# A GAT layer and a top-p attention layer on one core: layer 1's output shift added in layer 0, and single-column operations given from VectorE to GpSimd

## The chip, the cores and the metric

The kernel runs on one core of a Trainium2 chip. Its time is the device time of one execution in microseconds (us). A core has five engines that run at the same time, each with its own instruction queue that it works through in order: TensorE (PE, matrix products, whose weight loads are listed apart as PEld), VectorE (DVE), ScalarE (ACT), GpSimd (POOL) and SyncE (SP, which here issues DMA transfers only). An instruction that needs another engine's result waits on a semaphore, and everything behind it in its own queue waits with it. GpSimd also issues DMA transfers, from the same queue as its arithmetic.

## The reference

Two layers over a graph of 3327 nodes with 256 features. Layer 0 is a graph attention layer with four heads and a projection; layer 1 takes a normalised copy `h` of its result through two steps of a graph walk and of a sparse attention, sums them, normalises, scales by `ln_g`, shifts by `ln_b`, and adds the result to what came in:

```python
h = relu(layernorm(x))
x = x + gat(h, adj, weight, weight_u, weight_v, bias, proj_w, proj_b)     # layer 0
h = relu(layernorm(x))                                                    # layer 1
R = (adj + I) / row_sums
Z, Xf, Xa = 0, h, h
for n in range(2):
    A = top_p(softmax((Xa @ W1.T @ W2.T) @ (Xa @ W3.T).T))
    Xf = R @ Xf
    Xa = A @ Xa
    Z = Z + Xf @ U1[n].T + Xa @ U2[n].T
out = x + layernorm(h + Z) * ln_g + ln_b
```

`top_p` keeps in each row the largest probabilities until they reach 0.9 of the row's sum, sets the rest to zero and divides the row by what is kept.

## The kernel before

The 3327 nodes are 26 row tiles of 128 (the last has 127).

**Layer 0** goes through the transposed adjacency in four blocks of columns: three of 1024 and a narrow one of 255. In each of a block's 26 steps VectorE makes four weight tiles (`weigh`, L570, one for each head, into seven buffers `w`), two before and two after the other VectorE work of that step, and TensorE multiplies them with the features (`sum_features`, L578) and with a column for the denominators (`sum_weights`, L588). A block's 8 row tiles are finished while the next block runs, one every three steps; the last block's two are finished at the end of the layer. Finishing a tile is the class `Out`: TensorE transposes the sums (L437), VectorE's `normalize` divides them and adds the residue (L445 to L451: this is `x1`, the input of layer 1's residue), stores `x1` to `x1_d`, and takes its mean and variance (L457, L459); GpSimd makes the scale and the shift of the norm (L461 to L463), ScalarE applies them (L464: `h`), and TensorE turns `h` (L473) and makes queries and keys (L483) and the features of the graph walk (L506). VectorE comes back in `take_keys` (L178) and `take_graph` (L517). GpSimd also copies the adjacency to `adj_r` by DMA.

**Layer 1** runs two steps (s = 0 and 1) over the 26 row tiles. Several tiles are in work at once: `m` (logits and exponentials), `a` (search of the threshold), `b` (the cut), `c` (transposes and the product), `d` (storing). The order in which their parts are issued is written out by hand in `PLANS`: for each step one plan for the fill, one for the steady part and one for the drain. The word `graph` there stands for a share of the graph walk, four row tiles of the adjacency (L742, L743), with which TensorE is filled. After the program is built, the order of TensorE, VectorE, ScalarE and GpSimd is fixed as it was issued.

For one row tile: TensorE makes the logits (L799); VectorE and ScalarE copy them to SBUF (L810); ScalarE takes the exponentials and their sum (`exp`, L822, after GpSimd's three constants at L820); GpSimd works out a first guess of the threshold in 22 operations on single columns (`guess`, L838 to L859, whose L846 is what the first probe needs); ScalarE probes it four times (`probe`, L880; after the first, `go_on`, L888 and L889, makes the next point `at`). After each of the other probes VectorE narrows the bracket (`narrow`, L902 to L924); at the first narrowing it first sets the bracket's ends (L899). Then ScalarE makes the threshold (L930). VectorE sums what lies below it (`low`, L937, one pass over the row of 3327, its sum `below`), takes the largest eight of eight segments (`largest`, L946) and finds the last value that is kept (`last_kept`, L954 to L970): the sum of the row less `below` (L959, `sums[:, :1]`) starts a running sum (L960). GpSimd checks that the cut is certain (`make_sure`, L977 to L980). VectorE zeroes the rest of the row (`keep`, L985) and takes the reciprocal `rk` of what is kept (L989). TensorE transposes the row (L998), VectorE and ScalarE copy it back (L1008), TensorE multiplies it with the features (L1019), and VectorE scales by `rk`: in step 0 to `nxa` (L1037), from which TensorE makes the next step's features, in step 1 to the output's sum (L1040). The output is then normalised: VectorE takes mean and variance (L156, L158), adds epsilon (L160), GpSimd raises to -1/2 (L162), and VectorE applies mean and `ln_g` (L1082), then the scale and the residue `x1`, read back from `x1_d` (L1085), and the shift `ln_b` (L1086).

Between the two steps, `load_graph` reads the graph features of step 1 with 18 DMA transfers issued by GpSimd (`move_rows` with GpSimd's queue, L145). They are issued at the head of the iteration in which the last row tile is `b` and the one before it `c`; each waits for the stores of its part and for the buffer. `mean_of_keys` (L262) needs the keys of step 1, read back by SP as `k_sb` (L246).

In the fill plan of step 0 `b.keep` stands before `m.guess`; in all other plans with a guess it stands after it.

Of the kernel before, what the change touches and what calls it, by code (L numbers as in the profile page):

```python
# [10 lines left out]
FP = mybir.dt.float32  # L11
# [5 lines left out]
ALU = mybir.AluOpType  # L17
# [4 lines left out]
P = 128  # L22
D = 256
DC = D // P
# [3 lines left out]
DA = 64  # L28
# [26 lines left out]
def kernel(  # L55
# [85 lines left out]
    def move_rows(queue, dst, src, pn):  # L141

        for p0, p1 in ((0, pn // 16 * 16), (pn // 16 * 16, pn)):
            if p0 < p1:
                queue.dma_start(out=dst[p0:p1], in_=src[p0:p1])  # L145

    def row_of(pool, src, name, queue=nc.sync, tag=None):

        t = pool.tile([P, D], FP, tag=tag or name, name=name)
        queue.dma_start(out=t, in_=src.partition_broadcast(P))  # L150
        return t

    def mean_and_rstd(src, pn):

        st = small.tile([P, 6], FP, tag="ln_st", name="ln_st")
        nc.vector.bn_stats(st[:pn], src[:pn])  # L156
        mv = small.tile([P, 2], FP, tag="ln_mv", name="ln_mv")
        nc.vector.bn_aggr(mv[:pn], st[:pn])  # L158
        ve = small.tile([P, 1], FP, tag="ln_ve", name="ln_ve")
        nc.vector.tensor_scalar(ve[:pn], mv[:pn, 1:2], EPS, None, ALU.add)  # L160
        rs = small.tile([P, 1], FP, tag="ln_rs", name="ln_rs")
        nc.gpsimd.tensor_tensor(rs[:pn], ve[:pn], mhalf[:pn], ALU.pow)  # L162
        return mv, rs
# [138 lines left out]
    with ExitStack() as l0:  # L302
# [26 lines left out]
        load_x(4, 8)  # L329
        badd = row_of(p0, bias, "badd", nc.gpsimd)  # L330
        pb = row_of(pa, proj_b, "pb", nc.gpsimd, tag="xu")
        for g0 in range(8, NT, 4):
            load_x(g0, min(g0 + 4, NT))
        w1_sb = p0.tile([P, DC, DA], FP, name="w1_sb")
# [95 lines left out]
        class Out:  # L430
# [10 lines left out]
            def normalize(r):  # L441
                pn, i, pt = r.pn, r.i, r.pt
                rden = small.tile([P, H], FP, tag="rden", name="rden")

                nc.vector.tensor_scalar(rden[:pn], pt[:pn, HP, ::QP], 1.0 / BIG, None, ALU.max)  # L445
                nc.vector.reciprocal(rden[:pn], rden[:pn])
                x1 = pa.tile([P, D], FP, tag="x1", name="x1")
                for h in range(H):
                    hs = slice(h * O, (h + 1) * O)
                    q0 = (h % 2) * O  # L450
                    nc.vector.scalar_tensor_tensor(  # L451
                        x1[:pn, hs], pt[:pn, h // 2, q0 : q0 + O], rden[:pn, h : h + 1],
                        res[:pn, i, hs], ALU.mult, ALU.add,
                    )
                move_rows(nc.sync, x1_d[r.n0 : r.n0 + pn], x1, pn)
                st = small.tile([P, 6], FP, tag="ln_st", name="ln_st")
                nc.vector.bn_stats(st[:pn], x1[:pn])  # L457
                m = small.tile([P, 4], FP, tag="ln_m", name="ln_m")
                nc.vector.bn_aggr(m[:pn, :2], st[:pn])  # L459
                g = nc.gpsimd  # L460
                g.tensor_scalar(m[:pn, 2:3], m[:pn, 1:2], EPS, None, ALU.add)  # L461
                g.tensor_tensor(m[:pn, 2:3], m[:pn, 2:3], mhalf[:pn], ALU.pow)
                g.tensor_scalar(m[:pn, 3:], m[:pn, :1], -1.0, m[:pn, 2:3], ALU.mult, ALU.mult)  # L463
                nc.scalar.activation(  # L464
                    res[:pn, i], x1[:pn], AF.Relu, bias=m[:pn, 3:], scale=m[:pn, 2:3]
                )
                move_rows(nc.sync, h_d[r.n0 : r.n0 + pn], res[:, i], pn)
# [80 lines left out]
            features(i, (7, 1)[i % 2])  # L548
            take(i)

        w1n = p0.tile([DA, DC, P], FP, name="w1n")
        pt = bank(2, [P, DC, P])
        for c in range(DC):
            nc.tensor.transpose(pt[:DA, c, :], w1_sb[:, c, :], ident)
# [141 lines left out]

    pl = ctx.enter_context(tc.tile_pool(name="pl", bufs=1))
    lng = row_of(pl, ln_g, "lng")
    lnb = row_of(pl, ln_b, "lnb")

    def load_nodes(xa, s, g):

# [68 lines left out]
    class Rows:  # L771
# [113 lines left out]
        def go_on(r):  # L885

            pn = r.pn
            nc.scalar.activation(r.g[:pn], r.g[:pn], AF.Copy, scale=half)  # L888
            nc.scalar.activation(  # L889
                r.at[:pn, 4:], r.g[:pn], AF.Identity, bias=r.step[:pn], scale=r.per_g[:pn]  # L890
            )

        def narrow(r, j):

            pn = r.pn
            if j == 1:
                nc.vector.tensor_scalar(  # L899
                    r.ends[:pn, :, 1], far[:pn], r.at[:pn, 4:], None, ALU.add  # L900
                )
            nc.vector.scalar_tensor_tensor(  # L902
                r.at[:pn, 1:4:2], r.g[:pn].to_broadcast([pn, 2]), half,
                r.ea[:pn].to_broadcast([pn, 2]), ALU.mult, ALU.mult,
            )
            mk = small.tile([P, 2], U32, tag="mk", name="mk")
            nc.vector.tensor_tensor(mk[:pn], r.at[:pn, 1:3], r.at[:pn, 0:2], ALU.is_ge)
            nc.vector.copy_predicated(
                r.ends[:pn],
                mk[:pn].unsqueeze(2).to_broadcast([pn, 2, 2]),  # L910
                r.at[:pn, 3:].unsqueeze(1).to_broadcast([pn, 2, 2]),
            )
            fhi, nhi = r.ends[:pn, 1, :1], r.ends[:pn, 1, 1:]
            t = small.tile([P, 4], FP, tag="t", name="t")
            short, gap, w = t[:pn, :1], t[:pn, 1:3], t[:pn, 3:]
            nc.vector.tensor_tensor(gap, r.ends[:pn, 0], r.ends[:pn, 1], ALU.subtract)
            nc.vector.tensor_scalar(short, r.aims[0][:pn], fhi, 0.0, ALU.subtract, ALU.max)
            if j == PROBES - 1:
                nc.vector.scalar_tensor_tensor(
                    short, r.aims[1][:pn], fhi, short, ALU.is_gt, ALU.mult  # L920
                )
            nc.vector.reciprocal(w, gap[:, :1])
            nc.vector.scalar_tensor_tensor(w, gap[:, 1:], w, short, ALU.mult, ALU.mult)  # L923
            nc.vector.tensor_tensor(r.at[:pn, 4:], w, nhi, ALU.add)  # L924
# [9 lines left out]
        def low(r):  # L934
            pn, e = r.pn, r.e[: r.pn]
            r.below = small.tile([P, 1], FP, tag="below", name="below")
            nc.vector.scalar_tensor_tensor(  # L937
                r.lg[:pn, :N], e, r.th[:pn], e, ALU.is_lt, ALU.mult, accum_out=r.below[:pn]
            )

        def largest(r):

# [5 lines left out]
        def last_kept(r):  # L948
            pn = r.pn
            v8 = r.v8[:pn].rearrange("p s v -> p (s v)")  # L950
            v = small.tile([P, WINDOW], FP, tag="v", name="v", bufs=1)
            top = small.tile([P, 1], FP, tag="top", name="top")

            nc.vector.tensor_reduce(top[:pn], r.v8[:pn, :, 7], AX.X, ALU.max)  # L954
            nc.vector.max(v[:pn, :8], v8)
            nc.vector.match_replace(v8, v[:pn, :8], v8, -1.0)
            nc.vector.max(v[:pn, 8:], v8)
            sums = small.tile([P, WINDOW + 1], FP, tag="sums", name="sums", bufs=2)
            nc.vector.tensor_tensor(sums[:pn, :1], r.ssum[:pn], r.below[:pn], ALU.subtract)  # L959
            nc.vector.tensor_tensor_scan(  # L960
                sums[:pn, 1:], v[:pn], v[:pn], sums[:pn, :1], ALU.add, ALU.max
            )
            ends = small.tile([P, 2, WINDOW], FP, tag="vends", name="vends", bufs=1)
            for j in range(2):
                nc.vector.scalar_tensor_tensor(
                    ends[:pn, j], sums[:pn, j : j + WINDOW], r.tgt[:pn], v[:pn],
                    ALU.is_ge, ALU.mult,
                )
            r.vm = small.tile([P, 2], FP, tag="vm", name="vm")
            nc.vector.tensor_reduce(r.vm[:pn], ends[:pn], AX.X, ALU.max)  # L970
            r.found = sums, top
# [10 lines left out]
        def keep(r):  # L982
            pn, e = r.pn, r.e[: r.pn]
            kept = small.tile([P, 1], FP, tag="kept", name="kept")
            nc.vector.scalar_tensor_tensor(  # L985
                e, e, r.vm[:pn, 1:], e, ALU.is_ge, ALU.mult, accum_out=kept[:pn]
            )
            r.rk = small.tile([P, 1], FP, tag="rk", name="rk", bufs=4)
            nc.vector.reciprocal(r.rk[:pn], kept[:pn])  # L989


        def transpose(r, *groups):
# [87 lines left out]
        def store_output(r):  # L1080
            pn, zt = r.pn, r.zt[: r.pn]
            nc.vector.scalar_tensor_tensor(  # L1082
                zt, zt, r.mv[:pn, 0:1], lng[:pn], ALU.subtract, ALU.mult
            )
            nc.vector.scalar_tensor_tensor(zt, zt, r.rs[:pn], r.x1[:pn], ALU.mult, ALU.add)  # L1085
            nc.vector.tensor_add(zt, zt, lnb[:pn])  # L1086
            move_rows(nc.sync, out[r.n0 : r.n0 + pn], zt, pn)

    def general_cut(i, s, k_sb, pows):
# [387 lines left out]
```

## Time and profile before

| | us |
|---|---|
| median of 3 runs | 2095.51 |
| lowest and highest | 2094.33, 2095.57 |
| the profiled execution | 2095.06 |
| its span | 2092.8 |
| TensorE busy (95% of the span) | 1985.8 |
| VectorE busy (82%) | 1715.9 |
| ScalarE busy (60%) | 1265.2 |
| GpSimd busy (38%) | 787.5 |

The span is what the profiler's instructions cover; the rest of the execution's time lies around it. A row of a timeline gives start, duration, engine, line, operation, output and inputs, a count where rows are merged, and in brackets the time that the engine had been idle and what ended the wait. Matmuls overlap, so the busy time of TensorE is not a measure of how well it is used, but its idle time is time in which it had nothing to do. The column of the clock is the share of its full clock that TensorE was granted.

### The profile page before, as it was taken

Reading aid. Unit: us, or ns where it says so; the run is one execution under the profiler, and the core shown is the slowest. Engines: PE = TensorE matmul, PEld = TensorE weight load, DVE = VectorE, ACT = ScalarE, POOL = GpSimd, SP = SyncE. Lnnn points to the kernel's source line nnn. Section 1 sums busy time; section 2 is a strip of 40 time slices with the busy share of each in tenths; the row PEclk is TensorE's granted clock in tenths of the full one; section 3 lists DMA queues with packets and bytes.
Section 4 is the critical chain, followed back from the end, with each engine's and each line's share of the span. In section 5 each row is a group of like instructions: output and inputs, shape, how many; then the busy total and the mean of one; then the engine's idle time right before and its main releaser. Section 6 shows DMA issues by size and latency. Waiting matters only on the chain. (4 is left out here: it accounts for less than half of the span.)

```text
span 2092.8 us, 34266 instructions
## 1 busy us (share of the span) xinstructions
PE 1985.8 (95%) x11474; PEld 1387.5 (66%) x11474; DVE 1715.9 (82%) x4065; ACT 1265.2 (60%) x1940; POOL 787.5 (38%) x1834
## 2 busy tenths in 40 slices
PE   6999999999999679999999999998899999999996
PEld 3333223323333468888888888876798898888885
DVE  4777888878877388888888888864899999999995
ACT  2110000000012588888888888847899999999982
POOL 2330033223233233444444444432555444554441
PEclk9999999999999889999999999999899999999998
DMA  5455555655645433333333333377334443334420
GB/s 173 146 174 170 161 196 190 229 175 183 217 131 175 130 81 91 102 100 98 102 102 103 100 103 103 101 224 197 77 99 102 118 105 102 101 99 111 107 73 20
DMA packets 319569, 270.60 MB, mean 129 GB/s; under 512 B 30168, under 2 KB 293335, under 8 KB 319256
## 3 DMA queue, kind: packets, MB, share of 16 engines
q1 hardware_dynamic: 303480, 216.03, 37.7%
q0 software_dynamic: 14736, 51.62, 7.0%
q8 instruction: 92, 1.51, 0.3%
q14 instruction: 93, 0.76, 0.1%
q10 hardware_dynamic: 1168, 0.67, 0.1%
HBM read 177.79 MB, written 88.62 MB: 127 GB/s over the span
## 5 line engine op out<-in xcount | busy, mean ns | idle before, releaser
L880 ACT ACTIVATE junk<-lg,at 128x3327 fp8e4<-128x3327 f32 (+1 forms) x208 | 637.8, 3067 | 13.8 <-POOL at L846 11.2
L570 DVE SCALAR_TENSOR_TENSOR w<-xf,cf,at 128x1024 f32<-128x1024 f32 (+1 forms) x312 | 382.1, 1278 | 55.9 <-PE pt L588 55.9
L742 PE MATMUL accr<-xf,adjt 128*128 128x258 f32 (+3 forms) x1352 | 366.8, 304 | 19.3 <-DMA adjt<-adj_r 18.9
L578 PE MATMUL pt<-w,sup 128*64 128x512 f32 (+3 forms) x1456 | 341.0, 576 | 10.6 <-DVE w L570 8.5
L743 PE MATMUL accr<-xf,adjt 128*128 128x256 f32 (+1 forms) x1352 | 340.6, 284 | 0.0
L1019 PE MATMUL acca<-res,wt 128*128 128x256 f32 (+2 forms) x1352 | 319.3, 381 | 0.0
L1019 PE MATMUL acca<-xa,wt 128*128 128x256 f32 (+2 forms) x1352 | 315.1, 382 | 3.0 <-ACT wt L1008 3.0
L742 PEld LDWEIGHTS accr<-xf,adjt 128*128 128x128 f32 (+1 forms) x1352 | 259.0, 192 | 29.9 <-DMA adjt<-adj_r 14.3
L1019 PEld LDWEIGHTS acca<-xa,wt 128*128 128x128 f32 (+2 forms) x1352 | 251.1, 191 | 34.7 <-ACT wt L1008 3.5
L1019 PEld LDWEIGHTS acca<-res,wt 128*128 128x128 f32 (+2 forms) x1352 | 249.2, 191 | 30.8 <-issue 0.5
L743 PEld LDWEIGHTS accr<-xf,adjt 128*128 128x128 f32 (+1 forms) x1352 | 259.8, 192 | 5.6
L799 PE MATMUL pg<-k_sb,q 128*128 128x512 f32 (+2 forms) x728 | 242.5, 425 | 17.3 <-DVE lg L810 8.4
L578 PEld LDWEIGHTS pt<-w,sup 128*64 128x64 f32 (+1 forms) x1456 | 95.9, 136 | 221.4 <-issue 149.2
L820 POOL TENSOR_SCALAR sc<-sc 128x1 f32<-128x1 f32 (+1 forms) x156 | 29.2, 215 | 505.0 <-ACT sc L818 505.0
L998 PE MATMUL pt<-ident,e 128*128 128x128 f32 (+1 forms) x1352 | 193.4, 276 | 20.8 <-DVE e L985 13.5
L946 DVE MAX8 v<-lg 128x8 f32<-128x416 f32 (+2 forms) x416 | 210.0, 577 | 0.1
L998 PEld LDWEIGHTS pt<-ident,e 128*128 128x128 f32 (+1 forms) x1352 | 162.8, 144 | 61.2 <-ACT wt L1008 18.1
L937 DVE SCALAR_TENSOR_TENSOR lg<-e,th 128x3327 f32<-128x3327 f32 (+1 forms) x52 | 191.1, 3676 | 4.1 <-ACT th L930 4.1
L985 DVE SCALAR_TENSOR_TENSOR e<-e,vm 128x3327 f32<-128x3327 f32 (+1 forms) x52 | 191.2, 3677 | 0.1
L822 ACT ACTIVATE e<-lg,sc 128x3327 f32<-128x3327 f32 (+1 forms) x52 | 159.7, 3072 | 29.9 <-issue 27.4
L1008 ACT COPY wt<-pt 128x512 f32<-128x512 f32 (+2 forms) x268 | 142.6, 544 | 55.7 <-PE pt L998 39.0
L588 PE MATMUL pt<-w,eas 128*32 128x512 f32 (+3 forms) x1456 | 166.6, 569 | 0.0
(180 smaller groups left out, 2696.1 us busy)
## 6 DMA issues: line engine op xcount, KB each, us to landing
adjt<-adj_r SPq DMA_DIRECT2D x300, 256.0 KB, 3.2
at<-in_adj_t_dram SPq DMA_DIRECT2D x75, 512.0 KB, 3.8
adj_r<-at POOLq DMA_DIRECT2D x75, 512.0 KB, 4.7
qk_d<-qk SPq DMA_DIRECT2D x50, 128.0 KB, 2.2
q<-qk_d SPq DMA_DIRECT2D x100, 64.0 KB, 2.5
xf_d<-xf SPq DMA_DIRECT2D x50, 128.0 KB, 2.5
xf_d<-hl SPq DMA_DIRECT2D x25, 256.0 KB, 2.0
xf<-f_d SPq DMA_DIRECT2D x24, 256.0 KB, 4.9
```

The lines of the kernel that those rows point to most:

```text
L570: nc.vector.scalar_tensor_tensor(o, cb, cf[:pj, j, h : h + 1], a, ALU.max, ALU.mult)
L578: nc.tensor.matmul(acc[q * O : (q + 1) * O, :mn], sup[:pj, j, h * O : (h + 1) * O], ws[h][:pj, 512 * m : 512 * m + mn], start=(j == 0), st ...
L588: nc.tensor.matmul(acc[h * QP : (h + 1) * QP, :mn], eas[:pj, j, h : h + 1].to_broadcast([pj, QP]), ws[h][:pj, 512 * m : 512 * m + mn], sta ...
L742: nc.tensor.matmul(acc[:pn, :dx], w, xc[:, :dx], start=begin, stop=False)
L743: nc.tensor.matmul(acc[:pn, :D], w, xc[:, DX:], start=False, stop=end)
L799: nc.tensor.matmul(r.pg[p][:pn, :mn], r.q[:, v, :pn], k_sb[:, m0 : m0 + mn], start=(v == 0), stop=(v == 1),)
L880: nc.scalar.activation(junk[:pn], r.lg[:pn, :N], AF.Exp, bias=r.at[:pn, 4:], accum_out=r.g[:pn], saturate=False,)
L937: nc.vector.scalar_tensor_tensor(r.lg[:pn, :N], e, r.th[:pn], e, ALU.is_lt, ALU.mult, accum_out=r.below[:pn])
L946: nc.vector.max(r.v8[:pn, q], r.lg[:pn, q * w : min((q + 1) * w, N)])
L985: nc.vector.scalar_tensor_tensor(e, e, r.vm[:pn, 1:], e, ALU.is_ge, ALU.mult, accum_out=kept[:pn])
L998: nc.tensor.transpose(r.pt[g][: rows(c), j, : r.pn], r.e[: r.pn, c * P : c * P + rows(c)], ident[: r.pn, : r.pn],)
L1019: nc.tensor.matmul(r.acc[: r.pn], wt[: rows(c), j, : r.pn], xa[: rows(c), c, :], start=(c == 0), stop=(c == NT - 1),)
```

## The change

The shift `ln_b` is added to `x1` in layer 0, in `Out.normalize`, behind the variance: VectorE writes `x1b = x1 + ln_b` and that is stored to `x1_d` in place of `x1`. The addition at the end of layer 1 goes. `ln_b` is loaded in layer 0 by GpSimd's queue instead of by SP's at the start of layer 1. To make room, `w1n` shares the buffers of `x1`.

Five operations of VectorE on single columns (or two) become operations of GpSimd: epsilon in `mean_and_rstd`; the bracket's ends, issued in `go_on` instead of the first `narrow`; the start of the running sum, issued in `low` instead of `last_kept`; and `rk`, as a power of -1 instead of a reciprocal, in its place in `keep`.

```diff
@@ mean_and_rstd
-        nc.vector.tensor_scalar(ve[:pn], mv[:pn, 1:2], EPS, None, ALU.add)
+        nc.gpsimd.tensor_scalar(ve[:pn], mv[:pn, 1:2], EPS, None, ALU.add)
@@ layer 0, loads
         pb = row_of(pa, proj_b, "pb", nc.gpsimd, tag="xu")
+        lnb = row_of(p0, ln_b, "lnb", nc.gpsimd)
@@ Out.normalize
-                move_rows(nc.sync, x1_d[r.n0 : r.n0 + pn], x1, pn)
                 st = small.tile([P, 6], FP, tag="ln_st", name="ln_st")
                 nc.vector.bn_stats(st[:pn], x1[:pn])
                 m = small.tile([P, 4], FP, tag="ln_m", name="ln_m")
                 nc.vector.bn_aggr(m[:pn, :2], st[:pn])
+                x1b = pa.tile([P, D], FP, tag="xu", name="x1b")
+                nc.vector.tensor_add(x1b[:pn], x1[:pn], lnb[:pn])
+                move_rows(nc.sync, x1_d[r.n0 : r.n0 + pn], x1b, pn)
@@ layer 0, after the first ten row tiles
-        w1n = p0.tile([DA, DC, P], FP, name="w1n")
+        w1n = pa.tile([DA, DC, P], FP, tag="x1", name="w1n")
@@ layer 1, loads
     lng = row_of(pl, ln_g, "lng")
-    lnb = row_of(pl, ln_b, "lnb")
@@ go_on
+            nc.gpsimd.tensor_scalar(r.ends[:pn, :, 1], far[:pn], r.at[:pn, 4:], None, ALU.add)
@@ narrow
-            if j == 1:
-                nc.vector.tensor_scalar(
-                    r.ends[:pn, :, 1], far[:pn], r.at[:pn, 4:], None, ALU.add
-                )
@@ low
+            r.sums = small.tile([P, WINDOW + 1], FP, tag="sums", name="sums", bufs=2)
+            nc.gpsimd.tensor_tensor(r.sums[:pn, :1], r.ssum[:pn], r.below[:pn], ALU.subtract)
@@ last_kept
-            sums = small.tile([P, WINDOW + 1], FP, tag="sums", name="sums", bufs=2)
-            nc.vector.tensor_tensor(sums[:pn, :1], r.ssum[:pn], r.below[:pn], ALU.subtract)
+            sums = r.sums
@@ keep
-            nc.vector.reciprocal(r.rk[:pn], kept[:pn])
+            nc.gpsimd.tensor_tensor(r.rk[:pn], kept[:pn], minus1[:pn], ALU.pow)
@@ store_output
             nc.vector.scalar_tensor_tensor(zt, zt, r.rs[:pn], r.x1[:pn], ALU.mult, ALU.add)
-            nc.vector.tensor_add(zt, zt, lnb[:pn])
```

## The prediction

> **What bounds the kernel now.** I read the busy times stage by stage first, cut where the kernel's stages change: the adjacency blocks of layer 0 up to 620, the narrow last block and its end up to 700, the fill of step 0 of layer 1, its steady part, the change from step 0 to step 1, the steady part of step 1, the end.
>
> ```profile
> 100.00:620.00 520.00, 512.38 (x2806) 161.36 (x2798) 425.34 (x548) 48.79 (x144) 133.81 (x165) 1.00 0.55 182
> 620.00:700.00 80.00, 71.14 (x453) 30.24 (x452) 55.63 (x164) 17.67 (x48) 23.72 (x52) 0.96 0.53 156
> 700.00:800.00 100.00, 75.08 (x397) 63.74 (x397) 64.83 (x180) 77.40 (x105) 35.89 (x108) 0.86 0.39 101
> 800.00:1350.00 550.00, 549.10 (x3289) 480.55 (x3287) 479.29 (x1304) 483.65 (x720) 239.81 (x613) 1.00 0.39 101
> 1350.00:1500.00 150.00, 127.82 (x715) 106.19 (x714) 95.18 (x246) 99.50 (x144) 63.33 (x148) 0.94 0.60 169
> 1500.00:2000.00 500.00, 496.77 (x3049) 446.39 (x3048) 467.29 (x1324) 466.45 (x631) 237.44 (x631) 1.00 0.41 105
> 2000.00:2093.00 93.00, 72.82 (x408) 63.59 (x406) 68.76 (x182) 49.38 (x71) 23.99 (x54) 0.93 0.17 44
> ```
>
> After the stretch come TensorE, its weight loads, VectorE, ScalarE, GpSimd, the granted clock, DMA share, GB/s. TensorE fills both steady parts: 0.9 us of 550 idle, 3.2 us of 500. Relief of VectorE there is worth at most those 4.1 us. The change is decided where TensorE waits: the narrow block, the fills, the step change, the end. There I read the timelines engine by engine, beside the order of instructions in the two built programs: TensorE and ScalarE keep theirs; VectorE and GpSimd change as the diff says.
>
> **The step change.** GpSimd's timeline, then VectorE's:
>
> ```profile
> 1376.81 0.90 POOL L145 DMA_DIRECT2D xf<-xf_d  x1 [0.41 <-issue]
> 1379.83 6.78 POOL L145 DMA_DIRECT2D xf<-xf_d  x9 [2.12 <-issue]
> ...
> 1397.35 1.70 POOL L145 DMA_DIRECT2D xf<-xf_d  x3 [4.28 <-DMA xf_d<-hl]
> 1400.15 0.51 POOL L145 DMA_DIRECT2D xf<-xf_d  x1 [1.10 <-DMA xf<-xf_d]
> 1400.68 0.20 POOL L977 TENSOR_TENSOR sure<-sc,sums 127x1 f32<-127x1 f32 x1
> ```
>
> ```profile
> 1392.95 0.14 DVE L959 TENSOR_TENSOR sums<-sc,below 127x1 f32<-127x1 f32 x1
> 1393.13 0.25 DVE L960 TENSOR_TENSOR_SCAN sums<-v,sums 127x16 f32<-127x16 f32 x1
> ...
> 1394.05 3.68 DVE L985 SCALAR_TENSOR_TENSOR e<-e,vm 127x3327 f32<-127x3327 f32 x1
> ...
> 1398.52 0.48 DVE L1037 TENSOR_SCALAR nxa<-acca,rk 128x256 f32<-128x256 f32 x1 [0.58 <-PE acca L1019]
> ```
>
> GpSimd issues the 18 loads of the next step's graph features in order, each waiting for its stores or for an older load. The check of the last row tile (L977), ready at 1393.1, runs at 1400.68 because it is queued behind them. Nobody waits for L977. In the changed order the subtraction that makes `sums` stands at that very place, and VectorE's scan waits for it. Scan at 1400.68 + 0.19 (a one-column TENSOR_TENSOR on GpSimd, L856) + 0.05 = 1400.92 instead of 1393.13. From scan to the end of L985's accumulator is 4.61 us (1393.13 to 1397.74), so L985 ends at 1405.5; behind it on VectorE stands L1037 for row tile 24, now about 1405.6 instead of 1398.52: **+7.1 us**. For that TensorE waits (transposes of `nxa`, then all of tile 25). Moving `rk` adds to it: it stands ahead of the first load and waits for the L985 that ends at 1380.1, so that load starts near 1380.7, not 1376.81, and the ten loads end near 1388.3, not 1386.6. The DMA engines are full from 1384 to 1398, so I pass on 0.5 of these 1.7 us: +7.6, bounds 6.1 (the store of `hl` lands 1 us earlier among fewer loads) and 8.8.
>
> VectorE idles 11.6 us for `k_sb` before L262 at 1412.29, but that covers nothing: TensorE runs tile 25 from 1400.5 to 1416.5 without a gap that belongs to L262, and all of it slips.
>
> TensorE then stands still for about 8 us. What that does to its clock shows at 704, where it idled 6 us:
>
> ```profile
> 704.00:710.00 6.00, 0.19 (x2) 0.01 (x1) 0.55 (x1) 3.81 (x4) 2.34 (x9) 0.87 0.95 264
> 710.00:715.30 5.30, 5.28 (x21) 4.94 (x22) 0.62 (x1) 3.16 (x2) 4.47 (x17) 0.51 0.29 64
> 715.30:720.00 4.70, 4.70 (x34) 4.23 (x33) 2.62 (x6) 2.48 (x6) 0.13 (x1) 1.00 0.47 117
> ```
>
> 5.3 us at 0.51 of the clock lose 2.6 us of TensorE work. Some of tile 25's start waits for copies instead, so +2.0, bounds 0 and 2.7. The Trainium skill (TensorE: Matmul & The Clock Gate, What's actually happening) gives about 3.4 us of sustained work until full speed; by it the loss would be 1.7 us at most and the whole sum 0.3 us less, an estimate; the row says longer.
>
> **The shift in layer 0.** Each of 26 row tiles gets a 128x256 addition. L1086, the same addition, takes 0.425 us and the next instruction follows 0.34 us after its start (2030.45 to 2030.79); 0.34 is the price. In the wide blocks VectorE is 425 of 520 us busy and waits for free `w` buffers; seven of them cover the 16 tiles' 0.34 there. In the narrow block nothing does:
>
> ```profile
> 642.83 0.18 DVE L459 BATCH_NORM_AGGREGATE ln_m<-ln_st 128x2 f32<-128x6 f32 x1
> 642.93 1.24 DVE L570 SCALAR_TENSOR_TENSOR w<-cb_end,cf,at 128x255 f32<-128x255 f32 x3
> 643.44 0.83 PE L578 MATMUL pt<-w,sup 128*64 128x255 f32 x3 [0.27 <-DVE w L570]
> ```
>
> TensorE already waits 0.27 us for the `w` just behind the aggregate, and the addition goes between the two. VectorE is tied to TensorE at L517 of each round (it waits for ScalarE's copy of TensorE's result), so it cannot get ahead. Eight tiles fall here: +2.7, bounds 1.2 (only half of it shows) and 3.6 (8 x 0.45). At the end of layer 0 tile 24's addition precedes tile 25's normalisation, and TensorE waits for that (L473, 1.17 us at 690.23): +0.34, bounds 0 and 0.7; tile 25's own hides before L178. The store of `x1` moves from `x1` to `x1b` at the same place of SP's queue, 0.4 us later; behind it is the store of `h`, which waits for ScalarE 2 us longer anyway: nothing, up to 0.4 without that cover. The load of `ln_b` leaves SP (0.46 us at 701.3, ahead of the first adjacency loads of layer 1, for which TensorE waits 5.8 us): -0.2, bounds -0.46 and 0. It joins GpSimd's queue at about 4.3 (0.54 us, as `pb`), and GpSimd is idle until 15.14. `w1n` takes an `x1` buffer until four 0.28 us matmuls have read it: nothing, at most 0.6.
>
> **Single columns.** VectorE loses 52 x (0.221 L899 + 0.142 L959 + 0.164 L989) + 26 x (0.154 L160 + 0.425 L1086) = 42 us of layer 1. GpSimd gets 52 x (0.24 for `ends`, between L820's 0.215 and L845's 0.265; 0.19 for `sums`; 0.57 for the power of `rk`, as L839) + 26 x 0.24. In the steady parts TensorE is the bound: step 0 nothing; step 1 -0.3, bounds -2 and +1. Its waits there (3.2 us) are for ScalarE's logits copies, which VectorE frees only in part. In step 1 the new order on GpSimd is guess, `rk`, `ve`, L162; L162 ended at 1861.34 and its user L1085 began at 1862.31, so 0.97 us cover the added 0.86, and with VectorE 0.2 us early there is a wait of about 0.1 against 0.34 saved behind it. In the fill of step 0 `rk` of tile 0 stands before the guess of tile 2: that guess starts near 756.05 instead of 746.53, its `at` comes at 759.6 and the probe that used it at 759.33 slips 0.4; less 0.18 for `sums`, and both reach VectorE through L930: +0.3, bounds -0.2 and 0.8. Fill of step 1: -0.2. End: `ends` and `sums` leave the path to the L985 for which TensorE waits 4.0 us, -0.3; behind the last product L1086 goes (-0.52 with its gap) and `ve` on GpSimd costs 0.12 more before L162, -0.35; bounds of both together -0.9 and -0.3.
>
> The Trainium skill (SBUF — State Buffer, Who interferes with whom) says that a VectorE instruction with two SBUF inputs and a GpSimd instruction that reads SBUF exclude each other, the later one waiting for the whole of the other. That speaks against giving GpSimd more, and the trace agrees: L852 took 3.67 us under an L985 of 3.68. By it `ends`, issued at 1864.1 beside an L937 that ran from 1864.17, could come 3.4 us late, an estimate; its first user is at 1869.81, so the sum stays.
>
> **Sum:** 7.6 + 2.0 + 2.7 + 0.34 - 0.2 + 0.3 - 0.3 - 0.2 - 0.65 = +11.6. The profiled execution took 2095.06 (span 2092.8 and 2.3 around it), 0.45 under the median of the runs shown: 2106.7 on its scale, **2107** against the median.
>
> **Rivals.** (a) The stall at the step change is covered: tile 25 would have had to wait for something else near 1412 anyway. For it: VectorE's 11.6 us idle. Against: TensorE's unbroken work from 1400.5. The sum loses 9.6: 2097.5, no change; it decides if TensorE takes work ahead of tile 25. (b) Faster: in step 1 VectorE, 93% busy, is what makes ScalarE's copies late. Freed of 1.1 us a tile it gives back all 3.2 us, and with the end and the fills (-0.85) that is 2091; it needs also that the loads let `sums` pass and that the narrow block hides its additions, against the 7.5 us for which L977 waited in the same queue. (c) Slower still: GpSimd's one-column work costs what L842 does on average (1.05), so that `rk` and `ve` take 2.1 instead of 0.86 and L1085 waits 1.3 a tile, 1.0 net of L1086, with the logits copies behind it. It decides from where VectorE's spare 1.6 us of each 23.98 us tile does not lie behind that wait; half of 1.0 reaching TensorE on 25 tiles is +12: 2119. Against: L842's mean is made of those that met an L937 or L985.
>
> **Chances.** My forecast 0.76, (a) 0.09, (b) 0.05, (c) 0.10. The low bounds add up to +3.5, the high ones to +18: I take 2099 to 2113, which leaves out (b), (c) and most of (a). A change under 0.2% (4.2 us) cannot be told from none: faster 0.05, same 0.11 ((a) and the lowest of my own range), slower 0.84.
>
> **What would show it.** Right: L960 of tile 25 waiting 7 to 8 us for GpSimd while the loads run, TensorE idle some 8 us before the transposes of `nxa` and half clock after; in the narrow block waits of 0.61 instead of 0.27; steady parts unchanged (23.98 us a tile). Wrong: `sums` running before the loads, no idle stretch near 1400, or waits of VectorE for `ln_rs` in every tile of step 1.

## The result, and the profile after

The changed kernel takes 2114.81 us (median of four runs, 2113.76 to 2117.60) against 2095.16 (2094.33 to 2095.57) of the kernel before beside it: ratio 1.0096, 95% interval [1.0084, 1.0108], 19.6 us slower. The forecast had the sign; 2107 was 7.8 us too little, and 2114.8 lies above its range. The profiled execution took 2117.60 us (span 2115.4), 2.8 above the median.

The profile after, cut by stages as in the prediction. The cuts are put where the same work stands, so the growth of a stretch is what its stage lost: 6, 3, 0, 0, 14, 0 and 0 us.

```profile
100.00:626.00 526.00, 517.74 (x2811) 161.31 (x2804) 430.73 (x566) 49.62 (x146) 135.43 (x165) 0.99 0.54 180
626.00:709.00 83.00, 71.70 (x455) 30.33 (x453) 59.08 (x174) 17.69 (x48) 23.29 (x52) 0.96 0.51 154
709.00:809.00 100.00, 75.86 (x399) 63.98 (x399) 64.29 (x173) 77.85 (x105) 42.40 (x117) 0.86 0.38 99
809.00:1359.00 550.00, 549.13 (x3290) 480.36 (x3289) 471.76 (x1241) 484.00 (x720) 319.35 (x676) 1.00 0.39 101
1359.00:1523.00 164.00, 131.88 (x715) 109.51 (x714) 93.66 (x231) 99.63 (x144) 70.25 (x160) 0.91 0.56 154
1523.00:2023.00 500.00, 496.52 (x3047) 445.95 (x3046) 449.55 (x1219) 466.27 (x631) 329.85 (x715) 1.00 0.41 105
2023.00:2116.00 93.00, 73.00 (x407) 63.62 (x405) 65.02 (x163) 49.28 (x70) 34.94 (x68) 0.93 0.17 44
```

Both steady parts are what they were (550 and 500 us, with 0.9 and 3.5 us of TensorE idle against 0.9 and 3.2), although VectorE has 7.5 and 17.7 us less to do in them and GpSimd 80 and 92 us more. The loss lies in layer 0 and at the step change. Lines of the changed kernel: L574 and L582 are the weight tiles and `sum_features`, L462 the new addition, L941 the start of the running sum and L961 the scan, L986 `keep`, L990 `rk`, L1038 `nxa`.

GpSimd's timeline at the step change:

```profile
1388.66 0.57 POOL L990 TENSOR_TENSOR rk<-kept,consts 128x1 f32<-128x1 f32 x1 [3.81 <-DVE e L986]
1389.26 0.90 POOL L145 DMA_DIRECT2D xf<-xf_d  x1
1392.31 5.96 POOL L145 DMA_DIRECT2D xf<-xf_d  x8 [2.14 <-issue]
...
1411.13 0.52 POOL L145 DMA_DIRECT2D xf<-xf_d  x1 [0.96 <-DMA xf<-xf_d]
1411.66 0.20 POOL L941 TENSOR_TENSOR sums<-sc,below 127x1 f32<-127x1 f32 x1
```

VectorE's:

```profile
1411.90 0.25 DVE L961 TENSOR_TENSOR_SCAN sums<-v,sums 127x16 f32<-127x16 f32 x1 [10.89 <-POOL sums L941]
...
1416.43 0.48 DVE L1038 TENSOR_SCALAR nxa<-acca,rk 128x256 f32<-128x256 f32 x1
...
1423.29 3.35 DVE L262 TENSOR_REDUCE mean<-k_sb 128x1 f32<-128x3072 f32 x1 [4.50 <-DMA k_sb<-qk_d]
...
1437.55 0.48 DVE L1038 TENSOR_SCALAR nxa<-acca,rk 127x256 f32<-127x256 f32 x1 [10.64 <-issue]
```

TensorE's, and then the stretches of its stop and of what follows, with the granted clock third from the end of the row:

```profile
1416.97 0.69 PE L1048 MATMUL pt<-ident,nxa 128*128 128x128 f32 x2 [10.95 <-DVE nxa L1038]
```

```profile
1406.00:1416.90 10.90, 0.02 (x1) 0.00 (x0) 4.90 (x7) 0.00 (x0) 2.69 (x6) 0.70 1.06 311
1416.90:1420.40 3.50, 2.97 (x12) 2.57 (x13) 0.43 (x2) 0.77 (x3) 0.91 (x5) 0.50 1.00 197
1420.40:1423.80 3.40, 3.40 (x7) 1.77 (x7) 0.51 (x1) 1.31 (x3) 0.00 (x0) 0.50 0.59 152
1423.80:1427.00 3.20, 3.20 (x19) 2.62 (x18) 3.10 (x2) 0.49 (x2) 0.00 (x0) 0.98 0.00 0
```

The chain is the one foretold: L990 waits for L986 of tile 24, the loads begin behind it, `sums` of tile 25 stands behind the loads, the scan waits for it (10.89 us, not 7 to 8), TensorE stops and then runs 6.9 us at half clock. Measured from the start of L986 of tile 24 (1376.42 before, 1384.90 after) the `nxa` of tile 24 comes 9.4 us later than before, that of tile 25 another 3.1, and the first copy of step 1's logits is 12.6 us later in all (44.77 to 57.34 us). Up to L986 of tile 27 another 1.5 us is lost.

In layer 0 the narrow block shows the wait of 0.61 us that was foretold; TensorE's timeline:

```profile
632.33 1.04 PE L582 MATMUL pt<-w,sup 128*64 128x255 f32 x4 [0.61 <-DVE w L574]
```

But the wide blocks lose 0.33 us a tile too. From one tile's turn to the next's is 19.81 us before (331.06 to 350.87) and 20.14 after (333.50 to 353.64). TensorE shows hardly any idle time there (8.3 us of the first 526 above, 7.6 before), since the ends of matmuls are modelled and a matmul whose input is late counts as busy. The weight loads show it. Before, in the step in which a tile is normalised (VectorE's weight tiles on either side of the normalisation, then TensorE's loads):

```profile
295.64 3.68 DVE L570 SCALAR_TENSOR_TENSOR w<-xf,cf,at 128x1024 f32<-128x1024 f32 x3 [1.63 <-PE pt L588]
...
301.35 6.04 DVE L570 SCALAR_TENSOR_TENSOR w<-xf,cf,at 128x1024 f32<-128x1024 f32 x5
```

```profile
303.86 0.19 PEld L578 LDWEIGHTS pt<-w,sup 128*64 128x64 f32 x3 [0.27 <-DVE w L570]
```

and after:

```profile
305.96 0.26 PEld L582 LDWEIGHTS pt<-w,sup 128*64 128x64 f32 x3 [0.17 <-DVE w L574]
```

The step's first loads come 1.77 us later than before (303.88 against 302.11), the ones that wait for VectorE 2.10: 0.33 more. What they wait for is the second weight tile behind the variance. Before it was made by about 301.35 + 2 x 1.20 = 303.75 (1.20 us from one weight tile to the next), 0.11 ahead of the load; after by 303.43 + 2 x 1.20 = 305.83, 0.13 ahead. TensorE waited for that tile before the change as well, by next to nothing. VectorE's timeline of the changed kernel puts the addition in front of it:

```profile
303.12 0.39 DVE L462 TENSOR_TENSOR x1b<-x,lnb 128x256 f32<-128x256 f32 x1
303.43 4.87 DVE L574 SCALAR_TENSOR_TENSOR w<-xf,cf,at 128x1024 f32<-128x1024 f32 x4
```

and the 16 matmuls of that step take 4.01 us instead of 3.68 by TensorE's timeline. Sixteen wide tiles and the gap between the blocks make 5.0 us (1.1 over the kernel before ahead of the first such tile, 6.15 at the last).

### The profile page after: what moved, and what is told of

Same layout as the page of the kernel before. It is cut to its first block, busy times and chain, and to the rows that moved or that the text cites. A ratio compares the mean times of both kernels' runs of the same rounds, so it can differ in the third digit from the quotient of the medians.

```text
span 2115.4 us, 34325 instructions
## 1 busy us (share of the span) xinstructions
PE 1996.4 (94%) x11474; PEld 1390.0 (66%) x11474; DVE 1693.6 (80%) x3883; ACT 1265.9 (60%) x1940; POOL 985.5 (47%) x2017
## 4 chain that ended last, share of the span: by engine, by line
PE 76%; ACT 11%; DVE 6%; DMA 3%; issue 3%; POOL 1%; SPq 0%; DVEq 0%; POOLq 0%; ACTq 0%
PE acca L1020 22%; PE pt L582 15%; PE pt L592 7%; ACT junk L883 7%; PE pt L999 6%; PE pg L802 6%; PE accr L745 5%; PE accr L746 5%; PE pt L392 2%; PE pt L510 2%; PE pz L1063 2%; ACT e L825 2%; DMA adjt<-adj_r 1%; DVE w L574 1%; PE pt L390 1%
## 5 line engine op out<-in xcount | busy, mean ns | idle before, releaser
L574 DVE SCALAR_TENSOR_TENSOR w<-xf,cf,at 128x1024 f32<-128x1024 f32 (+1 forms) x312 | 382.4, 1279 | 56.3 <-PE pt L592 56.3
L582 PE MATMUL pt<-w,sup 128*64 128x512 f32 (+3 forms) x1456 | 348.0, 581 | 13.2 <-DVE w L574 11.3
L582 PEld LDWEIGHTS pt<-w,sup 128*64 128x64 f32 (+1 forms) x1456 | 96.3, 137 | 230.2 <-issue 152.5
L937 DVE SCALAR_TENSOR_TENSOR lg<-e,th 128x3327 f32<-128x3327 f32 (+1 forms) x52 | 191.2, 3676 | 4.9 <-ACT th L930 4.6
L986 DVE SCALAR_TENSOR_TENSOR e<-e,vm 128x3327 f32<-128x3327 f32 (+1 forms) x52 | 191.2, 3677 | 0.1
L895 POOL TENSOR_SCALAR ends<-consts,at 128x2 f32<-128x2 f32 (+1 forms) x52 | 151.9, 2921 | 42.5 <-ACT at L892 42.3
```

The source lines that it names most:

```text
L574: nc.vector.scalar_tensor_tensor(o, cb, cf[:pj, j, h : h + 1], a, ALU.max, ALU.mult)
L582: nc.tensor.matmul(acc[q * O : (q + 1) * O, :mn], sup[:pj, j, h * O : (h + 1) * O], ws[h][:pj, 512 * m : 512 * m + mn], start=(j == 0), st ...
L937: nc.vector.scalar_tensor_tensor(r.lg[:pn, :N], e, r.th[:pn], e, ALU.is_lt, ALU.mult, accum_out=r.below[:pn])
```

## The experiments

Each run stands beside the kernel before on the same chip; ratios are to it, with a 95% interval. The last column is the time from the start of L985 of tile 24 (L986 in the changed kernel) to the first copy of step 1's logits, from one profile each; 44.77 us in the kernel before, 57.34 in the changed one.

| run | median us | before us | ratio | step change us |
|---|---|---|---|---|
| e4_unchanged | 2113.83 | 2094.43 | 1.0095 [1.0078, 1.0112] | 57.42 |
| e1_sums_back | 2107.23 | 2094.43 | 1.0054 [1.0038, 1.0071] | 49.09 |
| e2_shift_back | 2104.85 | 2094.43 | 1.0050 [1.0034, 1.0067] | 57.27 |
| e3_rk_back | 2110.53 | 2094.43 | 1.0076 [1.0059, 1.0093] | 54.47 |
| e9_sums_rk_back | 2103.65 | 2096.15 | 1.0038 [1.0025, 1.0051] | 44.90 |
| e7_shift_late | 2097.76 | 2096.15 | 1.0006 [0.9996, 1.0016] | 45.13 |
| e6_shift_gpsimd | 2095.36 | 2096.15 | 0.9997 [0.9988, 1.0006] | 46.49 |
| e10_best | 2094.92 | 2096.15 | 0.9997 [0.9988, 1.0005] | 44.49 |
| e11_rk_alone | 2097.93 | 2092.72 | 1.0020 [1.0010, 1.0030] | 49.26 |
| e12_sums_alone | 2101.15 | 2092.72 | 1.0041 [1.0026, 1.0057] | 54.56 |
| e8_shift_twice | 2115.65 (one run) | 2092.72 | | |

**The changed kernel again.** No edit.

> The changed kernel once more, for a second profile and a closer time. The first profiled execution took 2117.6 us, 2.8 above the median of 2114.8, and its records show half clock after two short idle stretches (about 54 us and about 1451 us from the start) where the kernel before kept its full clock. Theory A (those two losses are chance, a matter of how the stretch falls): median again 2113 to 2116, and a profile in which at least one of the two stretches runs at full clock and which is 1 to 3 us shorter. Rival (they belong to the change): both at half clock again, at 2115 or more.

The ratio repeats (1.0095). The execution profiled took 2112.78 us, 4.8 less than the first one, yet both stretches are at half clock again, so theory A does not hold as put, nor the rival's 2115. What fell away is mostly a loss that I had not named, in the fill of step 0 (3.6 us; see the last section), and 1.2 us ahead of the first wide tile that is finished. The later runs settle the two that I had: half clock at 54 us is in every profile but that of the kernel before, and half clock at 1451 us, after a wait of 2.1 to 2.7 us for the adjacency, is in three of thirteen, with the step change as before in one of them (e10_best). So neither is tied to a part of the change. The step change is the same to 0.1 us in both profiles, and the wide blocks lose 0.33 to 0.34 us a tile in both.

**The start of the running sum back on VectorE.**

```diff
@@ low
-            nc.gpsimd.tensor_tensor(r.sums[:pn, :1], r.ssum[:pn], r.below[:pn], ALU.subtract)
@@ last_kept
+            nc.vector.tensor_tensor(sums[:pn, :1], r.ssum[:pn], r.below[:pn], ALU.subtract)
```

> The changed kernel, but the start of the running sum is taken by VectorE in last_kept as before; rk stays on GpSimd, so that the loads of the next step's graph features still start about 4 us late. Theory A (the stall at the step change is the wait for sums behind the loads, and the half clock follows from it): the scan of tile 25 waits for nobody, the nxa of tile 24 comes 9.4 us earlier against the rest, no half clock behind it: 12.5 less, 2102. Rival 1 (the late loads cost by themselves, since the graph share of step 1 needs them): only 7 to 10 less, 2105 to 2108, with TensorE waiting for xf or adjt behind 1420. Rival 2 (what the prediction worked out for this part, 9.6): 2105.

6.6 us less, 2107.2: the time of rival 1, but not by its mechanism, since behind 1420 TensorE has no wait for `xf`, and those for the adjacency are in every profile. The scan waits for nobody any more, and still 4.3 of the step change's 12.6 us remain (49.09 against 44.77). VectorE now waits 15.02 us for `k_sb` at L262, which lands at 1423.30, the same moment as in the changed kernel (1423.29), and the `nxa` of tile 25 is queued behind it. So the late loads have a price of their own.

**The shift back at the end of layer 1.**

```diff
@@ Out.normalize
-                x1b = pa.tile([P, D], FP, tag="xu", name="x1b")
-                nc.vector.tensor_add(x1b[:pn], x1[:pn], lnb[:pn])
-                move_rows(nc.sync, x1_d[r.n0 : r.n0 + pn], x1b, pn)
+                move_rows(nc.sync, x1_d[r.n0 : r.n0 + pn], x1, pn)
@@ store_output
+            nc.vector.tensor_add(zt, zt, lnb[:pn])
```

> The changed kernel, but the shift is added at the end of layer 1 as before and ln_b is loaded there; the five single-column moves stay. Theory A (the addition is paid in every row tile of layer 0, 14 in the wide blocks at 0.335 us and 3 us in the narrow block and behind it): 8 less in layer 0, 0.4 more at the end: 2107. Rival (the prediction: the wide blocks hide it, only the narrow block pays 3): 2112.

9.0 us less than the changed kernel beside it, as theory A has it and a little more. (The single-column moves that stay are four: epsilon, the bracket's ends, `sums` and `rk`.) The round of the wide blocks is back at 19.80 to 19.81 us (its deviation from the kernel before stays within 0.01 us over each block), so the wide blocks had hidden nothing.

**`rk` back on VectorE.**

```diff
@@ keep
-            nc.gpsimd.tensor_tensor(r.rk[:pn], kept[:pn], minus1[:pn], ALU.pow)
+            nc.vector.reciprocal(r.rk[:pn], kept[:pn])
```

> The changed kernel, but rk is VectorE's reciprocal again. Theory A (rk on GpSimd holds the first load back by 3.9 us, and 2.5 of these reach the last load, and with it sums): the scan of tile 25 waits 8.4 instead of 10.9 us, 2.5 less: 2112.3. Rival 1 (the prediction: the DMA engines are full, and only 0.5 passes): 2114.3. Rival 2 (rk and ve on GpSimd hold the output of each tile of step 1 back): the period of step 1 falls below 23.98 us and the time by more than 4.

3.3 us less than the changed kernel beside it. The scan waits 8.58 us, 2.3 less than 10.89, as theory A has it. The first load stands 0.65 us behind the start of L986 of tile 24 instead of 4.36, and the last one ends 24.4 us behind it instead of 26.8: of 3.7 us at the head 2.3 arrive at the tail. The period of step 1 does not change, which speaks against rival 2.

**Both back.** The two edits above together.

> The changed kernel, but both the start of the running sum and rk are VectorE's again; the shift in layer 0, the bracket's ends and epsilon stay as changed. Theory A (the loads of the next step's features start 4 us late because of rk, and everything that the step change loses hangs on that queue: sums behind it, or, without sums, the keys that land 11.6 us after the last load): first load 0.4 us after the L985 of tile 24 starts as in the kernel before, keys 11.6 us behind the last load, no wait for GpSimd; the step change costs nothing, and only layer 0's 6.7 is left, less 0.7 at the end: 6 over the kernel before, 2100.5. Rival 1 (sums is all, rk nothing): as with sums alone put back, 2107. Rival 2 (ends and epsilon cost on their own): over 2103.

The step change is the one of the kernel before (44.90 against 44.77 us); the rounds of the wide blocks take 20.14 us. What is left, a ratio of 1.0038 (5.2 to 10.7 us by its interval), holds layer 0's 8.0. The median is 3 us above the 2100.5 expected, inside the scatter of single executions (2099.1 to 2105.0 here), and just over the 2103 set for rival 2; but in this profile the distance to the kernel before stays between 6.9 and 7.9 us from the first tile of step 1 to the last but one, so ends and epsilon cost nothing that adds up.

**`rk` alone, and `sums` alone, in the kernel before.**

```diff
@@ keep
-            nc.vector.reciprocal(r.rk[:pn], kept[:pn])
+            nc.gpsimd.tensor_tensor(r.rk[:pn], kept[:pn], minus1[:pn], ALU.pow)
```

> The kernel before with nothing changed but rk, which is GpSimd's power in keep. Theory A (the late loads cost without sums too: the keys of step 1 land some 11.6 us after the last load, VectorE's mean waits for them, and the nxa of tile 25 is queued behind it): first load about 4 us later against the L985 of tile 24, keys about 2.5 later, nxa of tile 25 about 1.8 late and the clock at half behind it; 2 to 6 over the kernel before, 2098 to 2102. Rival 1 (with nobody waiting for sums the delay is hidden): 2096. Rival 2 (rk on GpSimd delays the output of each tile of step 1): the period of step 1 above 24.0 us.

> The kernel before with nothing changed but the start of the running sum, which GpSimd takes in low. Theory A (the whole cost is the one wait at the step change): the scan of tile 25 waits 8 to 8.6 us for GpSimd, TensorE idles about as long and runs the next 5 to 7 us at half clock, the steady parts keep their periods: 9 to 11 over the kernel before, 2105 to 2107. Rival (the wait is in every tile, as GpSimd is held up under VectorE's passes): waits of L960 for sums in many tiles and a period of step 1 above 24.0 us.

Moving `rk`, one instruction of 0.57 us, costs 5.2 us by the medians (2.1 to 6.3 by the interval of the ratio) and 4.5 at the step change, although nobody uses it for long. Through whom, VectorE's timeline shows, in the kernel before and then with `rk` alone moved:

```profile
1416.50 0.48 DVE L1037 TENSOR_SCALAR nxa<-acca,rk 127x256 f32<-127x256 f32 x1 [0.60 <-PE acca L1019]
```

```profile
1412.85 3.35 DVE L262 TENSOR_REDUCE mean<-k_sb 128x1 f32<-128x3072 f32 x1 [15.31 <-DMA k_sb<-qk_d]
1416.12 0.34 DVE L178 SCALAR_TENSOR_TENSOR qk<-pq,centres,qk 128x128 fp32r<-128x128 f32 x1
1416.38 0.47 DVE L1037 TENSOR_SCALAR nxa<-acca,rk 127x256 f32<-127x256 f32 x1
```

TensorE's with `rk` alone moved:

```profile
1416.91 0.69 PE L1047 MATMUL pt<-ident,nxa 127*128 127x127 f32 x2 [3.55 <-DVE nxa L1037]
```

This L1037, the `nxa` of tile 25, directly follows L178, where before 0.6 us lay between (1415.90 to 1416.50): it is held by the queue, not by TensorE. Measured from the start of L985 of tile 24 it comes 2.0 us later than before; the other 2.4 us of the 4.5 are lost behind it, where TensorE's clock is at 0.50 from 1416.9 to 1423.1. The keys land 11.0 to 12.2 us after the issue of the last load ended in all thirteen profiles (11.6 before, 11.9 here), wherever that load lies. That they come last because the loads are ahead of them in the DMA engines fits DMA shares of 1.0 and more in those stretches, but wasn't tried on its own.

`sums` alone costs 8.4 us by the medians, a little under the 9 to 11 expected, and 9.8 at the step change:

```profile
1398.36 0.27 DVE L961 TENSOR_TENSOR_SCAN sums<-v,sums 127x16 f32<-127x16 f32 x1 [7.88 <-POOL sums L941]
```

7.88 us is the wait worked out in the prediction for `sums` without `rk` (7.8). It is the only wait of this kind: in the steady parts VectorE does not wait for `sums`. The two do not add up (4.5 and 9.8, together 12.6): with both moved, the scan's wait runs while the keys are on their way, and in the changed kernel L262 and L178 are through at 1426.90, long before the `nxa` of tile 25 at 1437.55.

**The addition at another place, and on another engine.** Both in the kernel before, with the shift alone.

```diff
@@ Out.take_graph
+                x1b = pa.tile([P, D], FP, tag="xu", name="x1b")
+                nc.vector.tensor_add(x1b[:pn], r.x1[:pn], lnb[:pn])
+                move_rows(nc.sync, x1_d[n0 : n0 + pn], x1b, pn)
```

> The kernel before with the shift alone, but VectorE's addition is not put behind the variance but five steps later, ahead of the subtraction of take_graph, where VectorE idles 0.80 us for ScalarE's copy in wide and narrow blocks. Theory A (behind the variance VectorE is the bound, since four of the seven weight buffers are held until the sum of weights of their step and at most three tiles are ahead; ahead of take_graph it is not): a round of the wide blocks takes 19.81 us as before and one of the narrow block 9.17; with the addition gone from the end 0.4 less than before, 2094. Rival (VectorE has no room anywhere in these rounds, its idle stretches only mirror TensorE's pace): 20.14 and 9.51 as in the changed kernel, 2101.

> The kernel before with the shift alone, the addition made by GpSimd behind its three columns of the norm. Theory A (VectorE is what each round of layer 0 waits for): rounds of 19.81 and 9.17, 2094 as before or 0.4 less. Rival 1 (GpSimd's addition of 256 columns keeps VectorE from its weight tiles while it runs, 0.34 or more in each tile): rounds of 20.14 or longer, 2101 or more. Rival 2 (it makes the adjacency stores behind it in GpSimd's queue late, which nobody waits for in layer 0): as theory A.

In both, the round of the wide blocks takes 19.80 us and that of the narrow block 9.17 from turn to turn (9.00 the first one), as in the kernel before; both times are the same as before within their intervals. (The step change of 46.49 us in the second of them holds a wait of 2.32 us for the adjacency at 1379 with half clock behind it.) With the addition ahead of `take_graph`, VectorE's timeline shows it in a stretch that was idle:

```profile
334.16 0.42 DVE L517 TENSOR_TENSOR x1b<-x,lnb 128x256 f32<-128x256 f32 x1
335.05 0.42 DVE L520 TENSOR_TENSOR xf<-pt,xf 128x256 fp32r<-128x256 f32 x1 [0.47 <-ACT xu L511]
```

0.80 us of waiting for ScalarE has become 0.47. The same instruction costs 0.33 us a tile behind the variance and nothing in the round here. On GpSimd the addition takes 1.77 us by the median, against 0.42 on VectorE. It hardly touches VectorE's weight tiles: 16 of the 210 in the wide blocks' rounds, one in each round, take about 1.40 us instead of 1.28, and the round does not grow.

**The addition twice** behind the variance, into the same tile.

```diff
+                nc.vector.tensor_add(x1b[:pn], x1[:pn], lnb[:pn])
                 nc.vector.tensor_add(x1b[:pn], x1[:pn], lnb[:pn])
```

> The kernel before with the shift alone, behind the variance as in the change, the addition issued twice into the same tile. Theory A (VectorE has no slack there, in wide and narrow blocks alike): a round of the wide blocks takes 19.81 + 2 x 0.335 = 20.48 us and one of the narrow block 9.00 + 2 x 0.35 = 9.7 (from one turn to the next); the residue between the first wide turn and the narrow block is 10 us over the kernel before. Rival (there is some slack, which one addition used up): more than 0.335 for the second one, less for the first.

A round of the wide blocks takes 20.60 us and one of the narrow block 9.96: the first addition cost 0.33, the second 0.46 in both (it starts 0.43 us after the first, at its end, where a weight tile started 0.31 after it; it writes the same tile). Nothing is hidden, of one or of two. Of this run, a single execution, only the profile is used.

**What the runs left as useful.** The addition ahead of `take_graph`, the bracket's ends on GpSimd, `sums` on GpSimd except for the last tile of step 0, the rest on VectorE.

```diff
@@ low
+            g = nc.vector if r.s == 0 and r.i == NT - 1 else nc.gpsimd
+            g.tensor_tensor(r.sums[:pn, :1], r.ssum[:pn], r.below[:pn], ALU.subtract)
```

> What the runs so far leave as useful: the kernel before with the addition ahead of take_graph, the bracket's ends on GpSimd, the start of the running sum on GpSimd except for the last row tile of step 0, rk and epsilon on VectorE. Theory A (nothing of this waits): 0.4 from the addition and 0.3 to 0.9 from the shorter path to the last cut at the end: 2093.6 to 2094, which is hardly to be told from the kernel before. Rival (GpSimd's columns held up under VectorE's long passes make VectorE wait in the steady part): over 2096.

0.9997 [0.9988, 1.0005]: all of the change's loss is gone, and a gain over the kernel before can't be told from none. No version was found that is faster than the kernel before.

## Why the prediction was right or wrong

Term by term, on the profiled executions (22.6 us more in the span):

| step | predicted | measured |
|---|---|---|
| start, up to the first wide tile that is finished | 0 | +1.1 |
| wide blocks | 0 | +5.0 |
| narrow block and end of layer 0 | +3.0 | +3.0 |
| `ln_b` off SP, fill of step 0 | +0.1 | -0.6 |
| steady part of step 0 | 0 | 0.0 |
| step change up to `nxa` of tile 24 | +7.6 | +9.4 |
| half clock behind it | +2.0 | +3.1 |
| fill of step 1 | -0.2 | +1.5 |
| steady part of step 1 | -0.3 | +0.4 |
| end | -0.65 | -0.3 |

**Right:** that the step change decides, by `sums` queued behind the loads, with TensorE standing still and half clock after it; the narrow block, to the wait; that the steady parts don't care. Rival (c) had a point, but at another instruction: one of the four, the bracket's ends, takes far longer on GpSimd than the rows it was priced by (below), and it costs nothing; `sums` (0.19 us), epsilon (0.26) and `rk` (0.57) take about what they were priced at. What I had named as a sign against me, VectorE waiting for `ln_rs` in each tile of step 1, is there too, with 0.46 us a tile (9.7 over 21 tiles of the steady part by the waits of the changed kernel, where 0.1 was foretold); it does not reach TensorE.

**Wrong, first: "seven of them cover the 16 tiles' 0.34 there".** This is the largest miss, 5.0 us. Seven buffers are not seven tiles of lead: `sum_weights` reads all four tiles of a step at its end, so four are held until then, and VectorE waits for that (1.63 us until L588 at 295.64 in the kernel before). It gets three tiles ahead, spends the lead on the 2.1 us of normalisation, and delivers the second tile behind it just in time. 425 of 520 us busy is the average over places with slack and one without; the addition was put at the one without. Two runs that move it (19.80 us a round) and two that keep or double it (20.14, 20.60) show that it is the place; that the buffers set the lead is read from the wait for L588, and no run varied their number.

**Wrong, second: "so I pass on 0.5 of these 1.7 us".** The first load was rightly placed behind `rk` (foretold 1380.7 on the old scale, measured 1389.26 - 8.48 = 1380.8), but what becomes of the delay was not: the tenth load ended at 1398.67 + 0.75 - 8.48 = 1390.9 on that scale, not at 1388.3, and full DMA engines did not swallow the rest. Of the 3.7 us by which `rk` moves the first load, 2.3 reach the last one (`rk` back), where 0.5 was allowed. With 9.4 measured, the bound of 8.8 for this term was too low as well.

**What I had not seen:** that the keys land some 11.6 us behind the last load, with only 0.6 us to spare before `nxa` of tile 25. I had asked of VectorE's wait for `k_sb` only whether it covers anything, and not what makes it end. It doesn't show in the total, because the wait for `sums` is longer; but it is why putting `sums` back alone saves only 6.6 us.

**Mis-sized: "+2.0, bounds 0 and 2.7".** The half clock lasted 6.9 us after the 10.95 us stop, where the row that I took, after 5.8 us, has 5.3; it cost 3.1. The length of the stop is not what made the difference (last section).

The 1.1 us at the start is not there in the second profile of the changed kernel, and the fill of step 1 differs from the kernel before by -0.3 to +2.5 us over the other profiles, with half clock after waits for the adjacency that comes and goes with no part of the change; I count both as chance. The -0.6 of the fill of step 0 says little for the same reason: the second profile of the changed kernel has -4.2 there. By the parts that repeat, 8.0 in layer 0 and 12.6 at the step change, less about 0.5, the sum is 20; the medians say 19.6.

## What to carry to other kernels

Before something is moved to an engine that also issues transfers, look through its whole queue at the changes of stage, not at the steady part: one 0.2 us instruction behind 18 loads cost 8 to 10 us, and one 0.57 us instruction ahead of them 4 to 5, in a program whose steady parts gained and lost nothing. An engine's share of busy time says nothing of the place where an instruction is added: look for what the next consumer waits for there, in the weight loads where matmuls hide it, and put the instruction ahead of a wait. Buffers held until the end of a step are no lead.

## What the runs showed of the hardware

**A GpSimd instruction under a long pass of VectorE.** The bracket's ends, priced at 0.24 us, took 2.92 us on average; GpSimd's row for that line:

```profile
L895 POOL TENSOR_SCALAR ends<-consts,at x52: 296/3335/3881, 727.2 to 2054.2; 128x2 f32<-128x2 f32 x50, 127x2 f32<-127x2 f32 x2
```

It is issued at about the time of VectorE's L937 (3.68 us), and the median, 3.34, is nearly the whole of that pass. The Trainium skill (SBUF — State Buffer, Who interferes with whom) says that the one of the two that comes second waits for the whole of the other; this row agrees. It makes up 152 of the 198 us that GpSimd became busier by, and no engine waited for it.

**Half clock after short stops comes and goes.** In the fill of step 0 TensorE waits for the first tile of the adjacency. In the kernel before:

```profile
710.02 0.55 PE L742 MATMUL accr<-xf,adjt 128*128 128x258 f32 x1 [5.83 <-DMA adjt<-adj_r]
```

In the second profile of the changed kernel the wait at this place is 3.78 us, and the matmul behind it takes 0.36 us.

In four of the thirteen profiles the wait is 5.4 to 5.8 us and the first matmul takes 0.55 us, at half clock; in eight it is 2.1 to 3.9 us and the matmul takes 0.36. In the last (e8_shift_twice) a wait of 2.23 us has a matmul of 0.55 behind it, so the length of the wait alone does not decide. Long and short waits come with the shift in layer 0 and without it. In the first 100 us the mean clock was 1.00 in the profile of the kernel before and 0.98 in all the others, after a stop of 1.2 us in each. Such things move single executions by 2 to 4 us, so that a term of 1 us has to be read from milestones next to it, and not from the time. In the records of the clock in all thirteen profiles every stretch at half clock, but for the one at the program's end, lasts 3.41 us or two, three or four times that. At the step change, after stops of 3.3 to 11.3 us in seven profiles, TensorE worked at half clock for 5.5 to 7.0 us, and not longest after the longest stop.

The Trainium skill (TensorE: Matmul & The Clock Gate, What's actually happening) says that about 3.4 us of sustained work bring back the full clock. The stretches of the changed kernel above agree if only unbroken work is counted: 3.40 us at half clock in which TensorE was busy throughout, ahead of the full clock. But they stand behind another 3.50 us at half clock in which it was busy for 2.97. The whole lasted 6.9 us, twice the 3.4 us that the prediction's estimate by the page took for the whole.
